# Four fused layers on one core: the instruction lists ordered with another model of the machine

## The chip, the core and the metric

The kernel runs on one core of a Trainium2 chip. A core has five instruction streams: TensorE (PE in the profile, with its weight loads as PEld), VectorE (DVE), ScalarE (ACT), GpSimd (POOL) and SyncE (SP, which here issues most of the transfers). Each stream is a fixed list, worked through in order; the streams wait for one another by semaphores. Transfers between the chip's memory (HBM) and the core's on-chip memory (SBUF) run on 16 DMA engines. Matrix products land in a second on-chip memory, PSUM.

The metric is the device time of one execution in microseconds (us).

## What is computed

The input is a batch of 16 images of 192 channels and 32 x 32 positions, in float32. Four layers follow one another. Cut to what matters:

```python
# layer 0: a recurrent block (mLSTM) over the 1024 positions, with a 3x3 convolution behind it
h = layernorm(seq); x_in, z = split(h @ w_up + b_up)
x_act = silu(causal_conv(x_in)); q, k, v = x_act @ w_q, x_act @ w_k, x_in
m_new = max(log_f + m, i);  C = exp(log_f + m - m_new) * C + exp(i - m_new) * outer(v, k)   # per position
y = (norm(C q / denom) * mh_w + mh_b + skip * x_act) * silu(z) @ w_down
# layer 1: attention whose queries and keys are measured from 6-qubit circuits (64 amplitudes)
probs = abs(U @ encode(angles)) ** 2;  att = softmax(-dist(q, k) / tau) @ v
# layer 2: deformable 3x3 sampling: at each position 9 taps, 4 corners each, at offsets that a convolution gives
acc[c, tap] = sum over 4 corners of x[c, corner] * weight[corner]
# layer 3: 1x1 product, 2x2 Fourier weights, depthwise 3x3 convolution, gelu gate, 1x1 product
out = x + w_out @ (gelu(d[:510]) * d[510:])
```

## The kernel before

The whole program is one straight line of some 47,000 instructions without loops at run time. Python generators write it down: each generator emits the instructions of one layer and yields a number now and then, its cost so far, and `weave` always continues the generator that has used the smallest share of its total. So the order in which the program is written is an interleaving by hand. It has two phases with a barrier of data between them, since batch normalisation needs statistics of the whole batch.

Phase A (0 to about 3440 us) weaves three streams for each half image: `front` (normalise, project, gates), `chunks` (the recurrence in chunks of 128 positions) and `conv` (the convolution). Before it, `circuits` prepares the matrices of the quantum circuits with some 450 small DVE instructions.

Phase B (from about 3440 us to the end) weaves four: `vectors` (batch normalisation and the circuits' products, pcirc), `attention`, `layer2` and `layer3`. Each works on one of the 16 images, the later streams behind the earlier ones. The parts that the steps below speak of:

- `attention` computes the scores of a pair of heads twice. First (`largest`) PE writes pmax (L1146) and DVE takes its row maxima (mx, L1148). Then (`values`) PE writes pscore (L1185), ACT takes the exponential (pexp, L1188), and PE multiplies it with the values (pav, L1177). The maxima of the next pair are written between the exponentials of the present one.
- pmax, pscore, pcirc, paug and phad take turns in the same two PSUM buffers (tag big).
- `layer2_gathers` fetches for each tap and each 128 positions one gathered tile gt of 128 x 768 numbers with an indirect transfer that POOL issues (L1355), out of six buffers. ACT scales the first corner (acc, L1363), DVE adds the other three (L1396) and applies the tap's weight (L1398), PE sums the taps up in pdef (L1402). The text of it runs two taps ahead:

```python
1389        if n + 2 < len(taps):
1390            reads.append(read(n + 2))
1391        if n + 1 < len(taps):
1392            firsts.append(first(reads[n + 1]))
```

- `layer2_offsets` computes the offsets and weights (w, L1336) of an image with the product poffc (L1300); the image's gathers follow it.
- `layer3` is mostly DVE work: a depthwise convolution as multiply-adds (dc, L1498), then the product pout (L1533), added to the residual xo (L1526).

## Time and profile before

| | us |
|---|---|
| time, median of 3 runs | 9266.52 |
| lowest and highest of them | 9242.93 and 9267.09 |
| the profiled execution, its own time | 9250.15 |
| span of its instructions | 9248.3 |

| engine | busy us | share of the span | instructions |
|---|---|---|---|
| PE | 7865.4 | 85% | 30512 |
| PE weight loads (beside PE) | 3365.6 | 36% | 30512 |
| DVE | 6926.5 | 75% | 14313 |
| ACT | 4283.4 | 46% | 7433 |
| POOL | 1982.9 | 21% | 1680 |

The mean granted clock of TensorE is 0.904. The page's line of busy tenths, in 40 slices of 231 us each, shows the two phases (PE first, then DVE, ACT and the DMA engines):

```profile
PE   5999999999999969888888888888888888888853
DVE  7777777777777744767877778778678778778778
ACT  3444444444444425454544454454444545444432
...
DMA  1111111111111110533433433433333334334342
```

Each digit is the busy share of a slice in tenths, 9 standing for 90% or more. PE is nearly full in phase A and between 8 and 9 tenths in phase B; DMA traffic is light in phase A and three to four tenths in phase B, where the gathers run.

In the lines shown below, a line of waits names the engine and the instruction that waited, then the instruction that released it, then the us in total, the number of such waits and the longest of them. A line of the timeline has start, duration, engine, line of the kernel, operation, output and inputs, the count, and in brackets the idle time of the engine just before it with what ended it.

### The profile page before, as it was taken

To read this page: it belongs to the slowest core of one execution; us is meant where nothing else is said; L and a number is where in the kernel's file an instruction comes from. 1 tells how busy PE (TensorE), PEld (TensorE's weight loads), DVE (VectorE), ACT (ScalarE), POOL (GpSimd) and SP (SyncE) were. 2 spreads that over 40 slices of the span, in tenths; PEclk is the share of its full clock that TensorE was granted. 3 is DMA by queue.
4 is the path that set the end of the run, shared out by engine and by line. 5 is a ranking of instruction groups with operands and counts; after the bars stand their busy time and mean duration, and the time that the engine had idled before them with its cause. 6 is when DMAs were issued, how large, how long until landed. Compare 5 with 4: busy or idle time off the path is not lost. (4 is left out here: it accounts for less than half of the span.)

```text
span 9248.3 us, 91393 instructions
## 1 busy us (share of the span) xinstructions
PE 7865.4 (85%) x30512; PEld 3365.6 (36%) x30512; DVE 6926.5 (75%) x14313; ACT 4283.4 (46%) x7433; POOL 1982.9 (21%) x1680
## 2 busy tenths in 40 slices
PE   5999999999999969888888888888888888888853
PEld 2555555555555532232322222232223223232221
DVE  7777777777777744767877778778678778778778
ACT  3444444444444425454544454454444545444432
POOL 0100100101001100322322322322223223224342
PEclk9899999999999979999898898998898998999865
DMA  1111111111111110533433433433333334334342
GB/s 53 43 40 45 47 47 43 45 43 42 48 46 46 42 48 26 165 118 106 125 111 95 133 115 108 126 119 100 123 114 117 121 107 127 114 104 136 116 148 67
DMA packets 301028, 814.44 MB, mean 88 GB/s; under 512 B 47579, under 2 KB 164381, under 8 KB 300555
## 3 DMA queue, kind: packets, MB, share of 16 engines
q0 software_dynamic: 92160, 453.06, 15.7%
q1 hardware_dynamic: 208395, 355.55, 12.4%
q8 instruction: 239, 3.92, 0.2%
q14 instruction: 234, 1.92, 0.1%
HBM read 667.13 MB, written 132.94 MB: 87 GB/s over the span
## 5 line engine op out<-in xcount | busy, mean ns | idle before, releaser
L1355 POOL DMA_INDIRECT gt<-xg,ix x1152 | 1660.9, 1442 | 4098.2 <-DVE w L1336 1790.3
L1396 DVE SCALAR_TENSOR_TENSOR acc<-gt,w,acc 128x192 f32<-128x192 f32 x3456 | 1210.4, 410 | 171.3 <-ACT acc L1363 132.7
L1146 PE MATMUL pmax<-kt,qt 64*128 64x512 f32 x3072 | 1075.4, 682 | 229.0 <-ACT pexp L1188 125.4
L1148 DVE TENSOR_REDUCE mx<-pmax 128x2 f32<-128x1024 f32 x768 | 933.8, 1217 | 409.6 <-PE pmax L1146 403.2
L1185 PE MATMUL pscore<-qt,kt 64*128 64x512 f32 x3072 | 1056.2, 687 | 161.1 <-DVE mx L1148 73.9
L1188 ACT ACTIVATE pexp<-pscore 128x1024 f32<-128x1024 f32 x768 | 780.3, 1018 | 803.8 <-PE pscore L1185 801.0
L1177 PE MATMUL pav<-pexp,vo 128*64 128x512 f32 x3072 | 1003.9, 671 | 121.4 <-ACT pexp L1188 116.3
L1363 ACT ACTIVATE acc<-gt,w 128x192 f32<-128x192 f32 x1152 | 490.1, 450 | 1234.3 <-DMA gt<-xg,ix 1066.9
L509 POOL COPY qbd<-qT 32x384 f32<-32x384 f32 x512 | 305.2, 596 | 2837.7 <-PE se L543 2752.8
L1498 DVE SCALAR_TENSOR_TENSOR dc<-pad,wdw,dc 128x512 f32<-128x512 f32 x1152 | 804.3, 742 | 15.3 <-ACT dc L1496 14.8
L1402 PE MATMUL pdef<-acc,ident 128*128 128x384 f32 x1152 | 613.7, 619 | 176.9 <-DVE acc L1398 176.5
L539 ACT ACTIVATE dm<-dm,wtm 128x128 f32<-128x128 f32 x1536 | 490.7, 388 | 347.7 <-DVE dm L495 267.9
L1146 PEld LDWEIGHTS pmax<-kt,qt 64*128 64x128 f32 x3072 | 296.9, 198 | 831.0 <-issue 245.3
L1185 PEld LDWEIGHTS pscore<-qt,kt 64*128 64x128 f32 x3072 | 301.2, 200 | 694.9 <-issue 294.5
L551 PEld LDWEIGHTS pintra<-v,pt 128*128 128x128 f32 x3072 | 426.1, 212 | 163.3 <-issue 70.5
L1402 PEld LDWEIGHTS pdef<-acc,ident 128*128 128x128 f32 x1152 | 198.8, 215 | 660.1 <-DVE acc L1398 279.8
L551 PE MATMUL pintra<-v,pt 128*128 128x33 f32 x3072 | 435.3, 290 | 2.5 <-DVE pt L546 2.4
L1177 PEld LDWEIGHTS pav<-pexp,vo 128*64 128x64 f32 x3072 | 176.5, 142 | 699.5 <-issue 504.6
L546 DVE SCALAR_TENSOR_TENSOR pt<-se,dm 128x512 f32<-128x512 f32 x384 | 262.9, 685 | 141.0 <-PE se L543 137.9
L1052 ACT ACTIVATE prob<-pcirc 128x1024 f32<-128x1024 f32 x192 | 195.4, 1021 | 354.7 <-PE pcirc L1050 353.4
L543 PE MATMUL se<-qbd,kT 64*128 64x256 f32 x1536 | 291.4, 448 | 54.3 <-DVE pt L546 54.3
L1398 DVE TENSOR_TENSOR acc<-acc,wdef 128x384 f32<-128x384 f32 x576 | 317.1, 550 | 3.8
(424 smaller groups left out, 12660.6 us busy)
## 6 DMA issues: line engine op xcount, KB each, us to landing
dm<-gd SPq DMA_DIRECT2D x128, 768.0 KB
xg<-xt SPq DMA_DIRECT2D x224, 192.0 KB
gt<-xg,ix POOLq DMA_INDIRECT x1152
xb<-x_in SPq DMA_DIRECT2D x32, 384.0 KB
y<-ydram SPq DMA_DIRECT2D x32, 384.0 KB
x1d<-xb SPq DMA_DIRECT2D x32, 384.0 KB
xnd<-y SPq DMA_DIRECT2D x32, 384.0 KB
xn<-xnd SPq DMA_DIRECT2D x48, 256.0 KB
```

The costliest lines, as they stand in the source:

```text
L539: nc.scalar.activation(dm[:, h, :], dm[:, h, :], AF.Exp, bias=wtm[:, c, 64 + h:65 + h])
L551: nc.tensor.matmul(pa[:, hh * 33:hh * 33 + 33], pt[:, h * 128:(h + 1) * 128], v33[:, hh, :], start=True, stop=True)
L1146: nc.tensor.matmul(pm[:, hh, :], qT[r, tt * 128:(tt + 1) * 128], kT[r, hf * HS:(hf + 1) * HS], start=True, stop=True)
L1148: nc.vector.tensor_reduce(mx[:, tt, hf, :], pm, AX.X, ALU.max, negate=True)
L1177: nc.tensor.matmul(po[0][hh * 64:hh * 64 + 64], vo[:, tt, hh * 32:hh * 32 + 64], pe[:, hh * HS:(hh + 1) * HS], start=(tt == 0), stop=(tt = ...
L1185: nc.tensor.matmul(ps[:, hh * HS:(hh + 1) * HS], kT[r, tt * 128:(tt + 1) * 128], qT[r, s], start=True, stop=True)
L1188: nc.scalar.activation(pe, ps, AF.Exp)
L1355: nc.gpsimd.indirect_dma_start(out=gt, out_offset=None, in_=xg, in_offset=bass.IndirectOffsetOnAxis(ap=ix[:, c:c + 1], axis=0))
L1363: nc.scalar.activation(acc[:, j, :], gt[:, 0:192], AF.Copy, scale=w4[:, 0, c:c + 1])
L1396: nc.vector.scalar_tensor_tensor(acc[:, j, :], gt[:, cr * 192:(cr + 1) * 192], w4[:, cr, c:c + 1], acc[:, j, :], ALU.mult, ALU.add)
L1402: nc.tensor.matmul(po[:, 0:384], cn.ident, acc.rearrange("p j c -> p (j c)"), start=(t == 0), stop=(t == 8))
L1498: nc.vector.scalar_tensor_tensor(out, src, w, add, ALU.mult, ALU.add)
```

## The change

One argument of the context's constructor. With it, the scheduler described above plays the program through on another model of the machine. The usual model charges each instruction and each transfer a duration of its own. The other one keeps account of what is shared[...]. The rule by which the scheduler chooses is the same, and so is the text. What can change is the order in each of the five lists and, with it, which slot a tile gets and where semaphore waits stand.

```diff
@@ -1675,7 +1675,7 @@
     nc = bacc.Bacc("TRN2", target_bir_lowering=False, num_devices=1)
     d = {k: nc.dram_tensor(k + "_in", v.shape, F32, kind="ExternalInput").ap() for k, v in arrays.items()}
     out = nc.dram_tensor("out", [nb, 192, HW], F32, kind="ExternalOutput").ap()
-    with tile.TileContext(nc) as tc:
+    with tile.TileContext(nc, schedule_with_timeline_sim=True) as tc:
         network(tc, d, out, nb)
     r = run_bass_kernel_spmd(nc, [{k + "_in": v for k, v in arrays.items()}], core_ids=[0])
     return r.results[0]["out"].reshape(nb, 192, 32, 32)
```

## The prediction

> **What bounds the kernel now.** I read the table of stretches first, because the two halves of the kernel have different limits, then the waits of TensorE (PE), of ScalarE (ACT) and of VectorE (DVE) in the long second half, then the timeline of one such wait. The columns of the first view are: stretch, its length, busy time and instructions of PE, PE weight loads, DVE, ACT and POOL, granted clock, DMA share, GB/s.

> ```profile
> 0.00:150.00 150.00, 39.21 (x113) 24.16 (x115) 104.95 (x533) 27.46 (x31) 6.50 (x8) 0.97 0.16 48
> 150.00:3440.00 3290.00, 3031.26 (x13107) 1675.73 (x13105) 2360.76 (x4838) 1492.90 (x3146) 315.43 (x520) 0.93 0.14 46
> 3440.00:3800.00 360.00, 324.70 (x1415) 106.63 (x1413) 176.15 (x286) 172.92 (x229) 31.02 (x28) 0.97 0.19 58
> 3800.00:8500.00 4700.00, 4031.31 (x14506) 1392.09 (x14502) 3683.16 (x7431) 2307.04 (x3563) 1367.48 (x966) 0.91 0.38 118
> 8500.00:9248.30 748.30, 438.92 (x1379) 167.01 (x1379) 601.44 (x1229) 283.05 (x468) 262.45 (x158) 0.73 0.36 112
> ```

> PE idle time is length less busy: 110.8 us at the start, 258.7 in phase A (92% busy), 35.3 in the passage, 668.7 in the steady part of phase B (86% busy), 309.4 in the tail; together 1382.9 of the span. No order of instructions gets below PE's 7865.4 us of work, so a reordering can win only out of these five numbers, and half of it lies in 3800 to 8500. There, this is what PE waited for (us in total, times, longest):

> ```profile
> PE pmax L1146 <- ACT pexp L1188: 116.3, 70, 2.7
> PE pav L1177 <- ACT pexp L1188: 87.2, 33, 5.4
> PE pmax L1146 <- DVE mx L1148: 72.3, 72, 3.2
> PE pcirc L1050 <- DVE mx L1148: 63.7, 27, 4.8
> PE pscore L1185 <- DVE mx L1148: 63.4, 46, 2.9
> ...
> PE pscore L1185 <- ACT pexp L1188: 14.7, 16, 1.9
> ```

> With pcirc <- pexp 4.2 and phad <- mx 9.5 below them: 222.4 us behind ACT's exponentials and 208.9 behind DVE's maxima, 431 of the 669. And of ACT in the same stretch:

> ```profile
> ACT acc L1363 <- DMA gt<-xg,ix: 846.9, 373, 8.7
> ACT pexp L1188 <- PE pscore L1185: 641.7, 321, 9.8
> ACT prob L1052 <- PE pcirc L1050: 317.3, 126, 11.7
> ```

> ACT, only 49% busy here, stands 847 us at the first scaling of a gathered row, waiting for the gather. One case, in order of time:

> ```profile
> 5199.44 1.98 PE L1177 MATMUL pav<-pexp,vo 128*64 128x512 f32 x4 [5.32 <-ACT pexp L1188]
> ...
> 5204.20 0.46 ACT L1363 ACTIVATE acc<-gt,w 128x192 f32<-128x192 f32 x1 [4.81 <-DMA gt<-xg,ix]
> 5204.56 1.92 ACT L1188 ACTIVATE pexp<-pscore 128x1024 f32<-128x1024 f32 x2
> 5205.62 0.28 PEld L1177 LDWEIGHTS pav<-pexp,vo 128*64 128x64 f32 x2 [3.77 <-ACT pexp L1188]
> 5205.62 1.97 PE L1177 MATMUL pav<-pexp,vo 128*64 128x512 f32 x2 [2.19 <-ACT pexp L1188]
> ```

> The scaling sits ahead of the exponential in ACT's list; ACT idles 4.81 us, the two exponentials come after it, and PE idles 2.19 us for them. How long a gather takes, from the chain that ended last (start, us, what):

> ```profile
> 9033.41 4.50 DMA gt<-xg,ix
> ...
> 9059.23 6.68 DMA gt<-xg,ix
> ```

> [...] an exponential behind a waiting scaling does not pass it. [...] So I treat PE's busy time as what this order costs, not as a fixed quantity, but I price no gain inside it.

> **The change part by part.** It removes and adds no instruction of the kernel's text and no buffer; it moves instructions within the five lists. All of the effect is in waits.

> (1) Gathers. A model that gives a gather its queueing time should put the scaling (L1363) later in ACT's list and let ready exponentials go first. 222.4 us of PE's idle time is behind exponentials; not all comes from gathers, since exponentials are late also because ACT does other work. I take half, 111 us, as the gathers' share, and two thirds of that as removed, since the wait itself varies (2.27 us in the mean, up to 8.7): -74 us. Bounds: 0 (the model's gather is still too short) and -222. What is late next is DVE: the six multiply-adds behind each scaling pair (410 ns each, L1396) come later too, on an engine 78% busy.

> (2) Maxima. A maximum (1217 ns) frees the PSUM buffer that pmax, pscore and pcirc share. It is late where DVE's list puts ready side work ahead of it. If the list follows the chip better, a third of 208.9 goes: -70 us. Bounds: -140 and, if more side work gets ahead, +190 (worked out below).

> (3) Tail. PE waits little for itself here; DVE is busy 601 of 748 us and ACT waits 208.9 us for gathers. If half of DVE's 147 idle us were gathers met at the wrong time and half of those went: about -40. Bounds: -80 (DVE 90% busy: 601/0.9 = 668) and +40.

> (4) Phase A. PE is at 92% and the DMA share is 0.14, so the timing of transfers matters little. The largest PE waits are ph <- hc 71.8 and se <- pt 54.3. I take -20, bounds -90 and +90.

> (5) Start and the DMA lists. The 111 us of PE's idle time at the start stay: a load on SP's queue waits 81.0 us for the last tile of the circuits, whose memory it takes. POOL holds two kinds of instructions, head copies in phase A and gathers in phase B; its longest waits are for buffers to come free (2752.8 and 1515.2 us over the span) and for the weights of the next item (1790.3), so its order is given. SP's moved issues cost nothing while PE waits for no transfer after the first 150 us except one of 10.6 us; if that cover went, the first to suffer would be the broadcast loads dm, for which DVE now waits 9.8 us.

> (6) New stalls. Any fixed list meets a chip that departs from its model; the old list has its stalls in known places, the new one will have others: +55 us, a guess of a quarter of the gains of (1) to (4), which are 204; bounds 0 and +200.

> Sum: -74 - 70 - 40 - 20 + 55 = -149. The profiled execution took 9250.15 us (span 9248.3), 16 us under the median of 9266.52. 9250 - 149 = 9101, so **9100 us**, 1.8% under the median.

> **The rivals.** *More is won.* If the steady part of B reached phase A's 92%, it would take 4031/0.921 = 4377, -323; with (3) and (4) and without (6), about -385: 8865 us. For it: 431 us in two kinds of waits. Against: DVE would then be 84% busy, and its chains with PE have latencies of their own.

> *Slower: ready side work gets ahead of maxima.* A model with queues hands an engine its ready work early, before the urgent instruction is ready; on DVE that is multiply-adds of L1498 (742 ns) and L1396. If every one of the 768 maxima comes one such instruction later, 768 x 0.742 = 570 us of lateness; PE is exposed to it where it has nothing else ready, which I put at a third: +190. With 40 us of gains left, 9250 + 150 = 9400 us. It decides as soon as PE's waits behind maxima grow by more than the gain elsewhere, some 130 us, above 340 in the steady part. For it: DVE is 78% busy and such waits are already 209 us. Against: the rest of what PE could do is large, four streams interleaved.

> *No change.* Waits only move: ACT waits less for gathers, but gathers arrive no sooner, since POOL waits 1515 us for DVE to free their buffers; the sum of PE and DVE work decides: 9245 us. That the lists come out nearly the same belongs here.

> **How the numbers follow.** The forecast with its own range of 8970 to 9220: 0.42. More won: 0.15. No change: 0.09. Slower: 0.34. About 0.3% (28 us) is what a measurement of this kernel tells from no change. Faster 0.57, same 0.09, slower 0.34. The range reaches from a little below the rival of more won to a little above that of slower: 8820 to 9430.

> **What would show it.** Right: ACT's wait for gathers falls from 1066.9 us over the span to some 500 to 700; PE's waits behind exponentials in the steady part from 222 to about 150, behind maxima to about 140; phase A keeps its length within 60 us. Wrong: PE waits grow behind maxima, or the steady part of B gets longer while ACT's gather waits fall, or phase A moves by more than 90 us, which I have no mechanism for.

## The result, and the profile after

The changed kernel takes 9697.05 us (median of 4 runs, 9695.26 to 9708.12); the kernel before took 9254.96 us beside it (9242.93 to 9267.09). The ratio is 1.048, with a 95% interval of 1.046 to 1.0501: slower. The profiled execution has a span of 9694.6 us, 446 us more than before.

I cut both executions at the same events: the last statistics of phase A (L610), the first score (pscore), the last exponential (pexp), the end. The table of stretches of the kernel before, for phase A and for the stretch from first score to last exponential (called the steady part from here on):

```profile
150.00:3309.80 3159.80, 2969.95 (x12845) 1641.89 (x12841) 2301.30 (x4708) 1450.29 (x3087) 305.16 (x512) 0.94 0.13 44
3453.50:8816.70 5363.20, 4598.87 (x16763) 1577.13 (x16765) 4097.08 (x8213) 2625.20 (x4016) 1516.26 (x1068) 0.91 0.37 114
```

And of the kernel after, with its tail as a third line:

```profile
150.00:3475.20 3325.20, 3119.14 (x12841) 1708.89 (x12837) 2319.78 (x4706) 1462.69 (x3087) 306.54 (x512) 0.92 0.13 42
3624.90:9288.10 5663.20, 4543.66 (x16785) 1592.36 (x16785) 4152.17 (x8271) 2598.31 (x3989) 1353.54 (x1080) 0.87 0.36 109
9288.10:9694.60 406.50, 175.29 (x466) 83.05 (x466) 335.10 (x664) 124.20 (x216) 102.85 (x72) 0.63 0.32 100
```

The first number after the limits is the length. Phase A grew by 165 us, the steady part by 300; the tail shrank by 25 (431.6 to 406.5), the passage between the phases grew by 6. The reader should then compare PE's busy time, the first figure behind the comma. In phase A it grew by 149 of the 165 us although the same instructions run: PE does not wait more there, it works longer. In the steady part it fell by 55 while the length grew by 300. And the granted clock, third from the end, fell in both (0.94 to 0.92, 0.91 to 0.87). So waits alone do not describe this result. The trace gives the clock as stretches at 1 and stretches at 0.5. With them I split each part's length into three terms: PE's idle time; its work counted at full clock (busy time, each bit weighed with the clock granted then); and the rest, half of the busy time that fell into stretches at 0.5, called slow-clock loss.

| us | idle | work at full clock | slow-clock loss | length |
|---|---|---|---|---|
| phase A before | 190 | 2791 | 179 | 3160 |
| phase A after | 206 | 2886 | 233 | 3325 |
| steady before | 764 | 4174 | 425 | 5363 |
| steady after | 1119 | 3994 | 550 | 5663 |

Phase A: +16 idle, +95 work, +54 clock. Steady part: +355 idle, -180 work, +125 clock. What PE waited for in the steady part after (us, times, longest):

```profile
PE pscore L1185 <- DVE mx L1148: 316.1, 117, 9.0
PE pmax L1146 <- ACT pexp L1188: 130.7, 83, 10.3
PE pmax L1146 <- DVE mx L1148: 95.1, 71, 4.0
PE pav L1177 <- ACT pexp L1188: 77.8, 34, 6.0
PE pcirc L1050 <- DVE mx L1148: 70.7, 27, 4.4
PE pscore L1185 <- ACT pexp L1188: 66.5, 42, 4.8
```

Behind maxima (with smaller lines) 489 us, against 242 in the same part before; behind exponentials 333 against 270. What ACT waited for there:

```profile
ACT acc L1363 <- DMA gt<-xg,ix: 1119.3, 684, 12.2
```

And DVE:

```profile
DVE acc L1396 <- ACT acc L1363: 344.4, 309, 4.7
```

DVE's wait at a multiply-add for ACT's scaling was 121.5 us before. One case from the timeline of the changed kernel joins these waits:

```profile
5849.88 3.87 PE L1402 MATMUL pdef<-acc,ident 128*128 128x384 f32 x6
...
5856.37 0.46 ACT L1363 ACTIVATE acc<-gt,w 128x192 f32<-128x192 f32 x1 [4.71 <-DMA gt<-xg,ix]
5856.86 0.42 DVE L1396 SCALAR_TENSOR_TENSOR acc<-gt,w,acc 128x192 f32<-128x192 f32 x1 [3.98 <-ACT acc L1363]
...
5858.80 0.42 DVE L1396 SCALAR_TENSOR_TENSOR acc<-gt,w,acc 128x192 f32<-128x192 f32 x1 [1.52 <-ACT acc L1363]
...
5859.69 1.00 ACT L1188 ACTIVATE pexp<-pscore 128x1024 f32<-128x1024 f32 x1
...
5861.52 1.22 DVE L1148 TENSOR_REDUCE mx<-pmax 128x2 f32<-128x1024 f32 x1
...
5862.79 2.08 PE L1185 MATMUL pscore<-qt,kt 64*128 64x512 f32 x4 [9.04 <-DVE mx L1148]
```

A gather has not arrived. ACT stands 4.71 us at its scaling, DVE 3.98 us at the multiply-add behind that scaling. A maximum stands behind both in DVE's list, although its product was finished at 5844.82, before PE began the sums of taps (pdef) at 5849.88. It starts at 5861.52, and PE, whose next instruction needs the buffer that it frees, has idled for 9.04 us. The exponential at 5859.69 had its scores at 5849.94 and stood behind the scalings in the same way. That is the case of the prediction, made worse: the gathered work went further ahead of the chain (the attention's instructions pmax, mx, pscore, pexp, pav), not behind it.

The lists of instructions say the same. The table gives the place in an engine's list less the place in the text, as a median (plus is later than written), and how many pairs of half-array products stand next to each other in PE's list. (A half-array product uses 64 of PE's 128 rows or columns, 64*128 or 128*64 in the profile's lines. Two neighbours can share PE: at L267, in the groups shown further down, a product keeps PE busy for 0.56 us alone and for 0.28 with a neighbour.)

| | before | after |
|---|---|---|
| DVE: maxima L1148 | +14 | +65 |
| DVE: multiply-adds L1396 | -1 | -16 |
| ACT: exponentials L1188 | +12 | +22 |
| ACT: scalings L1363 | 0 | -13 |
| PE: pmax, pscore | 0, 0 | +9, +11 |
| PE: sums of taps, pdef | 0 | -37 |
| pairs of pmax, pscore, pav, of 768 | 654, 702, 686 | 768, 759, 766 |
| pairs of se, of 384 | 381 | 316 |
| pairs of plin, pz, pup at L267, of 96 | 64 | 18 |

One more fact of the lists corrects what stands above the prediction. There it says that the rule of choice is the same under both models. If the maxima are ranked 400 instructions earlier, the usual model moves them from 14 places behind the text to 5. Under the new model not one of some 41,800 instructions changes its place. So for this edit at least, how early an instruction is written does not count there. What the new model goes by in its place is not shown by any run.

### The profile page after: what moved, and what is told of

Same layout as the page of the kernel before. It is cut to its first block, busy times and chain, and to the rows that moved or that the text cites. A ratio compares the mean times of both kernels' runs of the same rounds, so it can differ in the third digit from the quotient of the medians.

```text
span 9694.6 us, 91844 instructions
## 1 busy us (share of the span) xinstructions
PE 7951.7 (82%) x30512; PEld 3444.1 (36%) x30512; DVE 6983.6 (72%) x14313; ACT 4256.0 (44%) x7384; POOL 1780.5 (18%) x1680
## 5 line engine op out<-in xcount | busy, mean ns | idle before, releaser
L1355 POOL DMA_INDIRECT gt<-xg,ix x1152 | 1456.4, 1264 | 4581.8 <-DVE w L1336 2211.5
L1396 DVE SCALAR_TENSOR_TENSOR acc<-gt,w,acc 128x192 f32<-128x192 f32 x3456 | 1272.5, 411 | 407.4 <-ACT acc L1363 368.5
L1148 DVE TENSOR_REDUCE mx<-pmax 128x2 f32<-128x1024 f32 x768 | 932.3, 1216 | 639.3 <-PE pmax L1146 631.2
L1185 PE MATMUL pscore<-qt,kt 64*128 64x512 f32 x3072 | 1013.1, 730 | 435.4 <-DVE mx L1148 316.1
L1146 PE MATMUL pmax<-kt,qt 64*128 64x512 f32 x3072 | 966.8, 714 | 273.9 <-ACT pexp L1188 130.7
L1188 ACT ACTIVATE pexp<-pscore 128x1024 f32<-128x1024 f32 x768 | 783.6, 1021 | 772.5 <-PE pscore L1185 768.7
L1363 ACT ACTIVATE acc<-gt,w 128x192 f32<-128x192 f32 x1152 | 511.8, 455 | 1309.9 <-DMA gt<-xg,ix 1231.5
L1177 PE MATMUL pav<-pexp,vo 128*64 128x512 f32 x3072 | 912.3, 674 | 87.4 <-ACT pexp L1188 77.8
L1498 DVE SCALAR_TENSOR_TENSOR dc<-pad,wdw,dc 128x512 f32<-128x512 f32 x1152 | 814.6, 742 | 0.9 <-ACT dc L1496 0.2
L1402 PE MATMUL pdef<-acc,ident 128*128 128x384 f32 x1152 | 566.3, 605 | 175.5 <-DVE acc L1398 162.5
L1185 PEld LDWEIGHTS pscore<-qt,kt 64*128 64x128 f32 x3072 | 280.1, 211 | 970.1 <-DVE mx L1148 426.4
L1146 PEld LDWEIGHTS pmax<-kt,qt 64*128 64x128 f32 x3072 | 270.3, 206 | 816.1 <-DVE mx L1148 242.2
L543 PE MATMUL se<-qbd,kT 64*128 64x256 f32 x1536 | 363.7, 476 | 116.4 <-DVE pt L546 116.4
L1402 PEld LDWEIGHTS pdef<-acc,ident 128*128 128x128 f32 x1152 | 221.2, 222 | 573.6 <-DVE acc L1398 253.3
L1177 PEld LDWEIGHTS pav<-pexp,vo 128*64 128x64 f32 x3072 | 162.0, 144 | 685.7 <-issue 545.9
L495 DVE TENSOR_TENSOR dm<-dm,causal 128x1536 f32<-128x1536 f32 x128 | 224.6, 1754 | 149.2 <-DMA dm<-gd 148.7
## 6 DMA issues: line engine op xcount, KB each, us to landing
xg<-xt SPq DMA_DIRECT2D x224, 192.0 KB
```

Of the source, the lines that this page charges most:

```text
L1146: nc.tensor.matmul(pm[:, hh, :], qT[r, tt * 128:(tt + 1) * 128], kT[r, hf * HS:(hf + 1) * HS], start=True, stop=True)
L1148: nc.vector.tensor_reduce(mx[:, tt, hf, :], pm, AX.X, ALU.max, negate=True)
L1177: nc.tensor.matmul(po[0][hh * 64:hh * 64 + 64], vo[:, tt, hh * 32:hh * 32 + 64], pe[:, hh * HS:(hh + 1) * HS], start=(tt == 0), stop=(tt = ...
L1185: nc.tensor.matmul(ps[:, hh * HS:(hh + 1) * HS], kT[r, tt * 128:(tt + 1) * 128], qT[r, s], start=True, stop=True)
L1188: nc.scalar.activation(pe, ps, AF.Exp)
L1355: nc.gpsimd.indirect_dma_start(out=gt, out_offset=None, in_=xg, in_offset=bass.IndirectOffsetOnAxis(ap=ix[:, c:c + 1], axis=0))
```

## The experiments

All ran beside the kernel before. Two edits recur. *Holding a list*: the program is laid out twice, and in the second layout each instruction of an engine gets an order edge (no wait) to the one before it in the first layout's list; the engines that are not held are laid out anew around it. *Ranking*: the scheduler's count of instructions is shifted around one statement, so that it counts as written earlier or later.

| run | us, median | ratio, 95% interval | phase A | steady | idle, work, clock loss in steady |
|---|---|---|---|---|---|
| e1 all lists old | 9274.75 | 1.0002 to 1.0027 | 3160 | 5357 | 774, 4172, 411 |
| e2 PE's old | 9886.08 | 1.0654 to 1.069 | 3390 | 5743 | 1017, 4159, 566 |
| e3 DVE's old | 10165.58 | 1.0951 to 1.0988 | 3826 | 5571 | 1096, 3997, 478 |
| e4 ACT's old | 9562.13 | 1.03 to 1.0334 | 3278 | 5523 | 1009, 3990, 524 |
| e17 SP's old | 9698.24 | 1.0465 to 1.05 | 3359 | 5625 | 1111, 4002, 513 |
| e5 ranks flat | 12082.21 | 1.302 to 1.3077 | 3762 | 7531 | 1102, 5666, 764 |
| e8 text | 12918.93 | 1.393 to 1.3977 | 5511 | 6656 | 1991, 3882, 783 |
| e6 maxima late | 9225.43 | 0.9957 to 0.998 | 3156 | 5331 | 930, 4062, 340 |
| e7 maxima early | 9172.51 | 0.9889 to 0.9922 | 3163 | 5275 | 749, 4198, 328 |
| e9 pairs | 9159.59 | 0.9872 to 0.9912 | 3160 | 5260 | 897, 3909, 455 |
| e10 pairs, maxima early | 9095.25 | 0.9808 to 0.9845 | 3157 | 5189 | 959, 3910, 321 |
| e11 pairs, maxima late | 9226.88 | 0.995 to 0.9977 | 3156 | 5348 | 1035, 3927, 385 |
| e12 new model, pairs | 9594.25 | 1.0347 to 1.0391 | 3224 | 5650 | 1083, 4001, 566 |
| e13 chain late | 9346.83 | 1.0048 to 1.0102 | 3163 | 5489 | 1077, 3969, 443 |
| e14 chain early | 9305.48 | 1.0028 to 1.005 | 3163 | 5407 | 1025, 3979, 402 |
| e15 chain early by 60 | 9272.61 | 0.9989 to 1.0025 | 3156 | 5371 | 951, 4043, 377 |
| e16 scores late | 9193.68 | 0.9884 to 0.9939 | 3156 | 5307 | 972, 3955, 380 |
| e18 gathers behind | 9681.45 | 1.0374 to 1.0488 | 3336 | 5597 | 1076, 4007, 514 |

**Which list costs (e1 to e4, e17).** I began with two theories: D, that DVE's list is the cause (side work ahead of maxima), and P, that PE's is.

```diff
-    with tile.TileContext(nc, schedule_with_timeline_sim=True) as tc:
-        network(tc, d, out, nb)
+    nc = program(arrays, True, keep(lists(program(arrays, False)), [mybir.EngineType.DVE]))
```

Here with DVE (e3); e2 has PE in its place, e4 Activation, e17 SP, e1 all five.

> The new model plans, but each of the five engines is held to the list that the usual model makes; only what is left to it (which of a tag's buffers a tile gets, and so some semaphore waits) can differ. If the loss sits in the lists: 9255 us within 0.5%, phase A ends at about 3310 us, first score to last exponential about 5363 us. If it sits in buffers and semaphores: above 9400.

> Only PE's list is held to the usual model's; the new model lays out the other engines around it. In the lists the maxima on DVE then stand 36 places behind the text in the median (14 before, 65 after). Theory P (PE's list is what costs: split pairs of half-array products in phase A, and sums of taps ahead of scores): 9300 or less, phase A back at about 3310 us. Theory D (DVE's list costs: ready side work ahead of maxima): phase A may mend, but the steady part keeps about half of its loss, 9400 to 9450, with PE waiting over 300 us behind maxima in it.

> Only DVE's list is held to the usual model's (maxima 14 places behind the text again); PE still gets scores and maxima products 3 to 4 places behind the text (9 to 11 after). Theory D: the steady part comes back to within 80 us of before, PE's waits behind maxima to 210 to 260 us, total about 9300 to 9350. Theory P: less than half of the loss comes back, 9480 or more, and phase A stays at about 3470.

> Only ACT's list is held to the usual model's (exponentials 12 places behind the text, 22 after; scalings of gathered rows at their places). The maxima on DVE stand 32 places behind the text. Theory ACT (scalings ahead of exponentials cost): below 9350. Theories P and D: between 9400 and 9600, since the maxima are still late and PE's list is still the model's.

e1 is the kernel before again (1.0015, at most 1.0027): the loss sits in the lists, and nothing else that the new model does matters beyond 0.3%. D and P both fell in this form: with DVE's or PE's list alone put back the kernel gets slower still. Phase A of e3 in the table of stretches:

```profile
150.00:3975.70 3825.70, 3419.82 (x12839) 1871.90 (x12837) 2297.75 (x4707) 1456.93 (x3086) 300.98 (x512) 0.84 0.11 37
```

It is 666 us longer than before, and DVE's busy time (third group) is the same as ever. Of the 666 us, 216 are PE's idle time, 108 work at full clock and 342 slow-clock loss. My reading is that the new model does not plan well around a list that is not its own; no run tests that reading. Only ACT's old list helped (-135 us, of which 140 in the steady part and 47 in phase A, with 45 given back in the tail). Its total of 9562 lies where D and P had put it, not below 9350, where a theory of ACT alone had it. So no single list carries the loss. e17 came later, with the question what of the steady part was still open:

> The new model, SP's list alone held to the usual model's; most of the other lists stay as in the changed kernel (PE has 15012 of 17024 instructions at the same place). If the issue order of the transfers makes the open 174 us: the steady part falls from 5663 to 5490-5560, total 9520 to 9600. If not: the steady part within 50 us of 5663, total 9650 to 9740.

The order in which SP issues transfers is not it.

**Is it the lost ranking (e5), or the distance from the text (e8)?**

```diff
@@ weave
             s[0] += next(s[2]) / s[1]
+            ts.cur_priority = start
```

That is e5, under the usual model. In e8 PE, DVE and ACT are held to the order of the text.

> The usual model and its times, but the place in the text no longer ranks the streams against each other: after each yield the count that ranks instructions is set back to where the weaving began. Maxima then stand 43 places behind the text (14 before, 65 after), the multiply-adds of the gathers 23 ahead of it (1 and 16). Theory R (the new lists are slow because ready work is taken as it becomes ready and the text's ranking is lost): 9550 to 9850, PE waiting about 450 to 550 us behind maxima in the steady part and a lower granted clock in both phases. Theory T (the new model's times for transfers and queues are what is off, ranking is kept): within 1% of before.

> PE, DVE and ACT work through the text as it is written, without any model. If distance from the text were what costs (theory X), this is at least as fast as before: 9260 or less. If a model's reordering is worth something and the new one's is only the wrong one, it is slower than before; by how much is not known, 9350 to 9900.

Both are far slower. e8 answers its question: the usual model's reordering is worth 3665 us over the text, so distance from the text is no harm in itself. e5 agrees with theory R in its sign, but is nearly five times as far off as it said at most, and in another way: in the steady part PE waits 648 us to sum up taps and 158 for maxima (R had 450 to 550), and its work at full clock rises to 5666 us, since only 275, 252 and 101 of 768 pairs of pmax, pscore and pav are adjacent. So it does not imitate the new model. It gave the next question: what is a pair worth?

**Pairs (e9, e12).** One statement of three in e9, and the edge of e12, which runs under the new model:

```diff
                 for hh in range(2):
                     r = slice(hh * 64, hh * 64 + 64)
+                    g.tc.trace_state.cur_priority -= 2000 * hh
                     nc.tensor.matmul(ps[:, hh * HS:(hh + 1) * HS], ...)
+                    g.tc.trace_state.cur_priority += 2000 * hh
@@ both (e12; full is the full-array product of the other tile)
-                nc.tensor.matmul(p[i], w[r, 1, ...], x[r, 1, :], start=False, stop=True)
+                half = nc.tensor.matmul(p[i], w[r, 1, ...], x[r, 1, :], start=False, stop=True)
+                tc.add_manual_dep(half.ins, full.ins.name, ...)   # order alone
```

> The usual model; the second product of each half-array pair of the attention (pmax, pscore, pav) ranks 2000 ahead, so that nothing stands between the two in PE's list: 768 of 768 pairs adjacent for each (654, 702, 686 in before; 768, 759, 766 after). Theory W (two neighbouring half-array products overlap on PE; split ones run one after the other): PE's busy time in the steady part, counted at full clock, falls from 4174 to about 4010 as after, and if PE sets the pace, the total to 9060-9130. Rival (the chain of buffers sets the pace, PE's saved time turns into idle time): 9200 or more.

> The new model, with one order added: in the products that come in two tiles (plin, pup, pz) a half-array product stands behind the full one of the other tile, so that its pairs are adjacent (96 of 96 and 64 of 64; 18 of 96 in the changed kernel). Theory W: phase A loses about 45 us of its 166 (plin took 139 us there against 96 before), PE's busy time in it falls by as much, total about 9650. Rival (pairs aren't what makes phase A's busy time longer): within 15 us of the changed kernel.

The half-array products of phase A in the groups of PE, of the kernel before (count, busy us, mean ns of one, idle time before):

```profile
L543 PE MATMUL se<-qbd,kT 64*128 64x256 f32 x1536 | 291.4, 448 | 54.3 <-DVE pt L546 54.3
...
L267 PE MATMUL pz<-hn,wup 64*128 64x512 f32 x128 | 54.7, 638 | 0.0
L267 PE MATMUL pup<-hn,wup 64*128 64x512 f32 x124 | 51.7, 641 | 0.0
L267 PE MATMUL plin<-x,wlin 64*128 64x512 f32 x124 | 35.0, 641 | 0.0
```

In the changed kernel:

```profile
L543 PE MATMUL se<-qbd,kT 64*128 64x256 f32 x1536 | 363.7, 476 | 116.4 <-DVE pt L546 116.4
...
L267 PE MATMUL pz<-hn,wup 64*128 64x512 f32 x128 | 70.7, 641 | 0.0
...
L267 PE MATMUL plin<-x,wlin 64*128 64x512 f32 x124 | 69.6, 641 | 0.0
...
L267 PE MATMUL pup<-hn,wup 64*128 64x512 f32 x124 | 51.7, 641 | 0.0
```

In e12:

```profile
L267 PE MATMUL pz<-hn,wup 64*128 64x512 f32 x128 | 36.1, 641 | 0.0
...
L267 PE MATMUL pup<-hn,wup 64*128 64x512 f32 x124 | 35.0, 641 | 0.0
L267 PE MATMUL plin<-x,wlin 64*128 64x512 f32 x124 | 35.0, 641 | 0.0
```

The mean of one product is 641 ns in all of them. But 124 of them keep PE busy for 69.6 us where each runs alone and for 35.0 where each has a neighbour: 0.56 against 0.28 us. So two neighbours run at the same time: together they take what one takes alone. In e12 PE's work in phase A fell by 105 us to 2781 and phase A by 101; the three groups at L267 make 86 of it (192.0 to 106.1). I had expected 45, having counted plin alone. e12's total is 103 us lower. But it does more than undo what the new lists tore: before, the three groups at L267 had 141.4 us, so 51 of the 86 were torn by the new lists and 35 are pairs that the kernel before did not have together either (64 of 96). The other part that the new lists tore is se (381 pairs to 316): its row grows by 72 us, of which 50 are work at full clock and the rest clock, and e12 leaves it (319 pairs, 366.7 us). So the two together, 51 and 50 us, account for the 95 us of added work in phase A; e12 wins about as much back, but in part elsewhere. The other 70 of the 165 us are slow-clock loss (54) and idle time (16).

In the steady part the same effect has the other sign. The products with the values (pav) and the last products of the circuits (pz, L1061, 128*32, which overlap further: in the kernel before one keeps PE busy for 0.12 us in the mean and lasts 598 ns) before:

```profile
L1177 PE MATMUL pav<-pexp,vo 128*64 128x512 f32 x3066 | 1002.4, 671 | 121.4 <-ACT pexp L1188 116.3 <-ACT pavc L1206 4.8
...
L1061 PE MATMUL pz<-prob,amat 128*32 128x512 f32 x720 | 86.6, 598 | 0.0
```

After:

```profile
L1177 PE MATMUL pav<-pexp,vo 128*64 128x512 f32 x3064 | 910.1, 674 | 87.4 <-ACT pexp L1188 77.8 <-ACT pavc L1206 5.0 <-issue 4.6
...
L1061 PE MATMUL pz<-prob,amat 128*32 128x512 f32 x720 | 201.0, 652 | 0.0
```

pav in e9, where all 768 pairs are adjacent, and in e5, where 101 are:

```profile
L1180 PE MATMUL pav<-pexp,vo 128*64 128x512 f32 x3066 | 907.0, 672 | 143.7 <-ACT pexp L1194 139.4 <-ACT pavc L1212 4.0
```

```profile
L1179 PE MATMUL pav<-pexp,vo 128*64 128x512 f32 x3064 | 1604.3, 674 | 88.1 <-ACT pexp L1190 78.7 <-ACT pavc L1208 8.6
```

From these two, a torn pair of pav costs (1604.3 - 907.0) / 667 = 1.05 us. For the 82 torn pairs of the kernel before that makes 993 us; its row has 1002.4. pmax, pscore and pav together gained 244 us in the changed kernel, and pz, which stood in eights before and in shorter groups after, lost 114 (0.12 us of PE's time each before, 0.28 after). e9 gives all of the first and none of the second: work falls by 265 us. Of that, 103 us reach the end of the steady part; 133 turn into idle time and 30 into slow-clock loss. PE sets the pace only in part: the total of 9160 lies between the two expectations.

**Maxima (e6, e7, e10, e11).** The sign and the presence of the pairs' edit vary:

```diff
+                g.tc.trace_state.cur_priority += 200
                 nc.vector.tensor_reduce(mx[:, tt, hf, :], pm, AX.X, ALU.max, negate=True)
+                g.tc.trace_state.cur_priority -= 200
```

> The usual model, one rank changed: the maxima L1148 rank 200 instructions later, so that they stand 42 places behind the text on DVE (14 before, 65 after). Phase A is untouched and ends at about 3310. Theory M (late maxima make the loss of the steady part): the steady part grows from 5363 to 5580-5660, PE's waits behind maxima from 242 to 430-500, total 9470 to 9560. Rival (PE has other work; late maxima are a symptom): below 9350.

> The usual model, the maxima L1148 ranked 200 instructions earlier (5 places behind the text instead of 14). Theory M: PE's waits behind maxima fall from 242 to about 170 and the total to 9190 to 9230. Rival: no change beyond 0.3%, or slower because what they pass (multiply-adds for sums of taps and buffers of gathers) is late next.

> Pairs adjacent, and the maxima ranked 200 earlier (5 places behind the text instead of 14). If the gain of early maxima (82 us alone) and that of pairs add: 8980 to 9050. If both only free PE from the same wait: as the better one alone.

> Pairs adjacent, and the maxima ranked 200 later (42 places behind the text). Against the run with pairs alone only the maxima differ now. Theory M (late maxima cost, and in the run with late maxima alone the cost was hidden by pairs that came together at the same time): 100 to 250 us above the run with pairs alone, PE idle 150 to 250 us more in the steady part. Rival (late maxima cost nothing): within 40 us of it.

e6 looked as if late maxima did no harm; it was 0.3% faster. The split shows why: idle time rose by 166 us, but work fell by 112, because more pmax and pscore pairs had come together (768 and 736), and the clock gave 85. With pairs held adjacent the series is clean: maxima 5, 14 and 42 places behind the text give 9095, 9160 and 9227 us. Lateness costs some 65 us for each step, less than M's 100 to 250 and more than nothing. e10 is 1.7% faster than before and so beats both kernels; it missed its 8980 to 9050, since the gains of e7 and e9 (0.9 and 1.1%) add only in part.

The waits, however, are not those that M names. Two lines of PE in the steady part of e9, then of e11:

```profile
PE pscore L1190 <- DVE mx L1150: 117.3, 77, 5.7
PE pdef L1408 <- DVE acc L1404: 62.0, 59, 2.1
```

```profile
PE pdef L1410 <- DVE acc L1406: 207.8, 76, 8.9
PE pscore L1192 <- DVE mx L1151: 99.7, 98, 4.1
```

From e9 to e11 all waits behind maxima grew from 306 to 337 us, but those for sums of taps from 62 to 209, and this is as much as PE's whole added idle time (139). In e6 it is the same (242 to 315 behind maxima, 41 to 205 for sums of taps). In the changed kernel the sums of taps cost only 62. So ranking maxima late costs time, but it does not make the changed kernel's waits.

**The whole chain (e13 to e16), and the gathers (e18).** Maxima alone leave most open: from e9 (5260) to the changed kernel (5663) the steady part has 403 us, and maxima 42 places late make 88, with other waits. In e13 all of pmax, mx, pscore, pexp and pav are ranked 200 later, under the usual model with pairs adjacent. e14 and e15 rank them 200 and 60 earlier, e16 is e13 with the maxima left at their rank.

> The usual model, pairs adjacent, and all instructions of the attention's chain (pmax, mx, pscore, pexp, pav) ranked 200 later. The lists' displacements are then those of the changed kernel: maxima 67 places behind the text (65 there), exponentials 25 (22), scores 15 (11), sums of taps 39 ahead (37). Theory C (the chain has lost its rank before filler): the steady part is 5600 to 5720 (5260 with pairs alone, 5663 in the changed kernel), PE idle 1050 to 1200 us in it, total 9480 to 9620 with phase A as before. Rival (transfers, gathers or buffers of the new model): the steady part stays below 5450, total below 9330.

> The same with the chain ranked 200 earlier (maxima 6 places ahead of the text, scores 4 ahead, sums of taps 16 behind). Theory C: no slower than the run with pairs and early maxima (9095), 9000 to 9095, unless the sums of taps and with them the gathers' buffers become late: then 9100 to 9250.

> The same with the chain ranked 60 earlier: between the run with pairs alone (9160) and the larger shift, 9020 to 9120.

> As the run with the whole chain late, but the maxima L1148 keep their rank (18 places behind the text in the median). If late maxima are most of the chain's effect: below 9250 and the steady part below 5350. If the whole chain counts: 9300 to 9450, between the run with pairs alone and the one with the whole chain late.

What PE waited for in the steady part of e13:

```profile
PE pscore L1192 <- DVE mx L1151: 248.6, 85, 9.5
PE pmax L1147 <- DVE mx L1151: 153.5, 138, 4.4
PE pmax L1147 <- ACT pexp L1197: 148.5, 105, 5.8
PE pscore L1192 <- ACT pexp L1197: 124.6, 57, 10.4
```

Compare the changed kernel above: the sums (mx 426 and pexp 344 us with smaller lines, there 489 and 333) and the idle time (1077, there 1119) are nearly those of the changed kernel. So the idle time can be made without the new model, by ranking the chain behind its filler. But the steady part is 5489 us, between the two expectations: 229 of the 403 us (of both figures some 33 come back in the tail). The open 174 are 42 idle, 25 work and 107 slow-clock loss. e16 stayed below the 9250 that it set for late maxima being most of the chain's effect. Yet e16 and e11 (34 and 67 us over e9 in total) make less together than e13 (187). It may be that the two kinds of lateness amplify each other; but the maxima stand 67 places behind the text in e13 and 42 in e11, so the two do not split e13 cleanly. e14 and e15 missed: the chain further ahead is no gain. PE then waits 415 and 392 us for exponentials (289 in e9), and in e15 its work rises by 134 us, much of it in the circuits' products pcirc (354.3 us busy, in e9 210.6).

e18 goes at the changed kernel itself, with order edges alone:

```diff
-                nc.vector.tensor_reduce(mx[:, tt, hf, :], ...)
+                g.newest.mx = nc.vector.tensor_reduce(mx[:, tt, hf, :], ...)
...
-                nc.vector.scalar_tensor_tensor(acc[:, j, :], gt[:, cr * 192:(cr + 1) * 192], ...)
+                add = nc.vector.scalar_tensor_tensor(acc[:, j, :], gt[:, cr * 192:(cr + 1) * 192], ...)
+                g.tc.add_manual_dep(add.ins, g.newest.mx.ins.name, ...)   # order alone
```

The same holds a scaling behind the newest exponential.

> The new model; on ACT a scaling L1363 stands behind the exponential written last before it, on DVE a multiply-add L1396 behind the maximum written last before it (order alone). Exponentials then stand 11 places behind the text (22 in the changed kernel), maxima 14 (65), scores 1 (11). Theory G (gathered work that the model believes ready stands ahead of the chain and blocks it): the steady part falls from 5663 to 5250-5450, DVE waiting at a multiply-add while PE idles from 120 to under 40 us, PE's waits behind maxima and exponentials together from 822 to under 650; phase A stays at 3475; total 9290 to 9490. Rival (sums of taps become late instead, 18 places behind the text, and gathers with them): 5600 or more.

The chain is back at the text (maxima 14 places behind it, scores 1), and PE's waits moved. Behind maxima and exponentials together they fell from 821 to 598 us, below the 650 that theory G had asked for. Two lines of the steady part:

```profile
PE pmax L1147 <- DVE mx L1149: 216.0, 110, 7.7
PE pdef L1407 <- DVE acc L1403: 194.1, 115, 7.3
```

Sums of taps were 60 us before the edit. DVE's idle time at a multiply-add while PE idles fell only from 120 to 84, and the steady part by 66 us to 5597: the rival's value but for 3 us. Most of that came back in the tail (452 us, 406 before the edit), and the total fell by 16. So gathers ahead of the chain are a visible way in which the new lists lose time, but setting them behind it moves the waits to the sums of taps and wins next to nothing.

**What stays open.** For the 174 us I can name what they consist of, mostly lower clock, and what they are not (SP's order; maxima, scores or gathers alone). Where the new model lays out PE's, DVE's and ACT's lists (the changed kernel, e12, e17, e18), the slow-clock loss of the steady part is 513 to 566 us; under the usual model, with the text's ranks or shifts of them (e6, e7, e9 to e11, e13 to e16), it is 321 to 455. e1 has the lists of the kernel before, and its three terms differ from that kernel's by 10, 2 and 14 us; a difference of that size means nothing, but one of 107 stands well above it. Which order among the other three engines' lists makes it was not found. Nor does a run show why the new model orders the lists as it does.

## Why the prediction was wrong

**Step (1), gathers.** Wrong in sign. The scalings went 13 places ahead of the text and the exponentials 22 behind it; ACT's wait for gathers rose from 1066.9 to 1231.5 us over the span (500 to 700 predicted), PE's behind exponentials in the steady part from 270 to 333. The mechanism of the step, a scaling that blocks an exponential, is in the trace. That a model with transfer queues would judge gathers better was an assumption, and the places and the timeline above speak against it: the lists put gathered work where it has not arrived.

**Step (2), maxima.** Wrong in sign as well: 242 to 489 us in place of a third less. The slower rival had the sign, and the mark it set (above 340) was passed. Its mechanism is in the trace, but how much it costs by itself is not shown: it gave +190 to late maxima, where e11 over e9 shows 88 us in the steady part, mostly for sums of taps; only the whole chain late (e13) makes 229. Its total of 9400 fell 297 us short. Over the whole span PE's idle time grew by 360 us where the rival had 150, the slow-clock loss by 175 where it had nothing, and work at full clock fell by 89.

**Step (3), tail.** Right in direction, -25 us for -40 (in a shorter stretch, from the last exponential on), but by luck: DVE's idle time, from which the 40 were to come, fell by 6 us there, and its work by 19, since less of it was left for the tail.

**Step (4), phase A.** +165 us against -20 with bounds of 90. I reasoned that phase A has few transfers, so that a model of transfers changes little. The lists there changed all the same, and the cost came where I had priced nothing: 95 us of PE work in products torn apart (at L267 and se) and 54 of clock. I had written that I had no mechanism for a move of more than 90 us; torn pairs are one.

**Step (5)** held: the start is the same, and e17 shows that SP's list is worth nothing. DVE's wait for the loads dm, which I named as the first to suffer, did rise from 9.8 to 148.7 us, without PE's idle time in phase A rising by more than 16.

**Step (6), new stalls.** +55 us with a bound of 200. PE's idle time rose by 355 us in the steady part alone.

The step that failed first stands ahead of the six: "All of the effect is in waits." Together with "I price no gain inside" PE's busy time, it left two of three terms out of the sum. PE's work moved by +95 and -180 us, the slow-clock loss by +54 and +125. "No order of instructions gets below PE's 7865.4 us of work" is wrong for the same reason: in e10, an order of the same instructions, PE is busy for 7494 us. In the steady part, where most of the loss is, the third term, waits, failed by its sign: steps (1) and (2) rested on a list that follows the chip better, chosen by an unchanged rule, and idle time rose by 355 us. The rank that moved nothing under the new model speaks against the unchanged rule, and ranks count in this kernel: alone, in e7 and e10, they move the time by 1 to 2%, and in e5 by 30%. That the lost ranking makes the loss is shown in part, by e13's 229 of 403 us in the steady part; the rest stays open.

Two small points, on which nothing rests: the two gathers that were timed at 4.50 and 6.68 us lie in the tail, where the DMA share is 0.36, and not in the steady part with its 0.38; and PE waits for a second transfer after the first 150 us, for 1.3 us.

## What to carry to other kernels

Where a kernel is tuned by the order of its text, first find out whether a scheduler still heeds that order: rank one urgent instruction earlier and see if it moves. Before pricing waits, split the bounding engine's time into idle time, work at full clock and slow-clock loss: this reordering moved all three (+355, -180 and +125 us in the steady part), and an edit that seemed harmless (late maxima, e6) was three effects that nearly cancelled (+166, -112 and -85 us). Look at which waits an experiment makes, not only at its total: late maxima cost time here, but not by waits behind maxima. Rank the second of two half-array products ahead, so that pairs stay together: with early maxima it made this kernel 1.7% faster.

## What the hardware showed that I had not expected

A stall of PE went with a loss beyond its length: 4.63 us of wait, and 5.25 us of slow-clock loss in a stretch at 0.5 that began within it. Phase A of the changed kernel, products of one kind before and after the stall, from the timeline:

```profile
1794.33 0.70 PE L543 MATMUL se<-qbd,kT 64*128 64x256 f32 x4
...
1797.90 1.14 PE L543 MATMUL se<-qbd,kT 64*128 64x256 f32 x4
...
1802.93 0.68 DVE L546 SCALAR_TENSOR_TENSOR pt<-se,dm 128x512 f32<-128x512 f32 x1
...
1803.66 1.23 PE L543 MATMUL se<-qbd,kT 64*128 64x256 f32 x4 [4.63 <-DVE pt L546]
```

The same time in the table of stretches:

```profile
1785.00:1798.00 13.00, 12.30 (x72) 7.89 (x69) 9.76 (x19) 5.61 (x11) 2.64 (x4) 1.00 0.21 45
1798.00:1803.66 5.66, 1.04 (x4) 0.49 (x4) 5.38 (x11) 1.60 (x5) 0.29 (x1) 0.82 0.34 132
1803.66:1812.00 8.34, 7.20 (x31) 5.80 (x31) 5.05 (x9) 2.85 (x11) 2.01 (x4) 0.50 0.00 0
```

PE works 1.04 of 5.66 us, and then for 8.34 us at a clock of 0.50; four products of se in two pairs take 1.23 us in place of 0.70. (The four at 1797.90 ran at full clock as well, but not as pairs; their starts lie 0.12 to 0.32 us apart.) The stretch at 0.5 lasts 13.65 us in all (1801.65 to 1815.30), and PE is busy for 10.50 us of it, which makes the 5.25 us of loss. The trace of the changed kernel has 265 stretches at 0.5, and all last multiples of 3.41 us, within 0.07. PE worked 0.80 of the 3.41 us before this one, and the full clock came back 11.6 us after the end of the stall. What begins such a stretch and what ends it was not shown. Nor does the loss follow the sum of idle time: early maxima (e10 over e9) left PE 62 us more idle and still saved 71 in the steady part, because 134 us of slow-clock loss went.
